# A mixture of experts with PE's order written out: two blocks interleaved by chunks, and the first layer's chunks in alternating PSUM banks

## The chip, the cores and the metric

One core of a Trainium2 chip runs the whole program in one launch. The metric is the time of one execution on the device in microseconds, as the median of several runs.

## The reference

The program is a network of four layers, each with a cross attention, a sequence block and a feed-forward block, on 16 x 64 = 1024 rows of 256 numbers, all in float32. The change touches only the feed-forward block of the second layer, a mixture of eight experts in which each row goes to its best two:

```
probs = softmax(xt @ gate_w.T)
top_w, top_i = top_k(probs, 2)
top_w = top_w / (top_w.sum(-1) + 1e-9)
h = gelu(einsum('td,ndh->tnh', xt, w1) + b1)       # 256 -> 1024
out_all = einsum('tnh,nhd->tnd', h, w2) + b2       # 1024 -> 256
out = (out_all at the chosen two, times top_w).sum(1)
```

The reference computes all experts for all rows; the kernel computes only the chosen ones.

## The kernel before, in words

The kernel is written on a layer that builds instructions for every engine, orders them by a scheduler, and sets the semaphores between engines from what each instruction reads and writes. `set_order(True)` and `in_order` add a chain between the instructions of one engine that are recorded through `mm`, `tr` or a `queue`, so that they stand in the order in which the program names them; without it the scheduler chooses the order.

`ffn1` (the method that the change edits) works so:

- The gate's logits, the two best experts of each row and the places of the rows are worked out by `choose` and by the lines after it. The 2048 choices (1024 rows times 2) are packed by expert into blocks of 128 places, with each expert's part rounded up to a whole block. NG = 23 blocks always suffice, and all 23 are computed. `whose` holds, for each block, which expert's weights it uses.
- `slots` turns places into lists: `src` (the row that stands at each place), `to` (where its result goes) and `weight`. Its matrix products are named `pi`, `pb`, `pw` and `pf`, and two of its inputs, `at` and `val`, are made on POOL.
- For each block, POOL issues indirect DMAs that gather the weights of the block's expert, `up` (128 x 2056, of which 8 columns are the bias) and `down` (128 x 2048), about 1 MB each, into three buffers each, and the block's 128 rows `xg` (`take`), also three buffers.
- `expert` then computes the block. Two transposes on PE put the rows into `pxg`, and DVE copies them to `xT`. The first layer's 1024 outputs are made in eight chunks of 128. A chunk is two products on PE (k = 0, 1) into its eighth of the PSUM tile `pu`, and one GELU on ACT from there into `hT` (L2631). The tile `pu` is 128 x 1024 float32, which is two PSUM banks: chunks 0 to 3 lie in the first and chunks 4 to 7 in the second. The second layer is eight products into `pd`, one for each chunk of `hT`. DVE scales the result by `weight` into `y` (L2637), and POOL scatters it to the table `d_y` in memory by an indirect DMA (L2642).
- A float32 product is two records in the profile, so a block has 32 `pu`, 16 `pd` and 2 `pxg` records on PE.
- There are two `pu` tiles (`big`, two buffers), and four PSUM buffers of one bank for `pxg`, `pd` and others (`mid`).
- The last block is not scattered. `add_sent` waits until all scatters have landed, loads the table back in eight pieces (`yk`, on SP's queue), adds the two halves of each on POOL, adds them to the residual `X` on DVE, and adds the last block by a product with a 0/1 matrix (`py`). The next stage begins with the statistics of `X`, and then transposes it (`psT`).

In the block loop the order is left to the scheduler: `set_order(False)` has been called at the end of `slots`. The scheduler puts the `pd` products of a block between its own `pu` chunks, and moves the next block's transposes and first chunks up into the present block. On POOL it issues the requests for `up`, `down` and `xg` in an order of its own; before the first block it puts two slot operations (L72 `at` and `val`) after the first three weight requests.

Of the kernel before, what the change touches and what calls it, by code (L numbers as in the profile page):

```python
# [8 lines left out]
F32 = mybir.dt.float32  # L9
U8 = mybir.dt.uint8  # L10
AF = mybir.ActivationFunctionType
ALU = mybir.AluOpType
# [3 lines left out]
P = 128  # L16
B, TQ, D = 16, 64, 256
N = B * TQ
# [37 lines left out]
def bc(ap, axis, n):  # L56

    ap = ap.unsqueeze(axis)
    shape = list(ap.shape)
    shape[axis] = n  # L60
    return ap.to_broadcast(shape)
# [17 lines left out]
class Net:  # L79
# [2663 lines left out]
            )  # L2743

    def ffn1(self):
        nc, a = self.nc, self.a
        L = "L1_ffn"

        NG = 2 * N // P + 7
        I32 = mybir.dt.int32  # L2750
        wg = self.w(a[f"{L}_gate_wT"].rearrange("(k p) n -> p k n", p=P), [P, 2, 8], "wg")
        with ExitStack() as es:
            one, two, big, mid = self.moe_pools(es, L)
            d_x, d_y = self.rows_dram(es, L)
            self.no_rows(d_y, one)
            row = self.numbers(one)
            comb = self.empty_combine(one)
            val = self.empty_values(NG, one)
            self.norm_T(mid, "m")
            p, oh, pq, seen, prod, gate = self.choose(wg, d_x, one, mid)  # L2760
            dve, pool = self.queue("dve", nc.vector), self.queue("pool", nc.gpsimd)

            pn = mid.tile([P, 512], F32, tag="m", name="pn")
            self.mm(pn[:, :8], self.ones, seen[:, :, 2 * NT - 1])
            over = one.tile([P, 8, 2 * NT], F32, name="over")
            fill, base, end = (one.tile([P, 8], F32, name=n) for n in ("fill", "base", "end"))
            below = one.tile([P, 8, 8], F32, name="below")
            dve.tensor_tensor(over, bc(self.nth[:, : 2 * NT], 1, 8), bc(pn[:, :8], 2, 2 * NT), ALU.is_lt)
            dve.tensor_reduce(fill, over, AX.X, ALU.add)
            dve.tensor_scalar(fill, fill, float(P), None, ALU.mult)  # L2770
            dve.tensor_tensor(below, self.lt8, bc(fill, 1, 8), ALU.mult)
            dve.tensor_reduce(base, below, AX.X, ALU.add)

            done = one.tile([P, NG, 8], F32, name="done")
            of = one.tile([P, NG], F32, name="of")
            whose = one.tile([P, NG], I32, name="whose")
            dve.tensor_tensor(end, fill, base, ALU.add)
            dve.tensor_tensor(done, bc(end, 1, NG), bc(self.nth[:, :NG], 2, 8), ALU.is_le)
            dve.tensor_reduce(of, done, AX.X, ALU.add)
            dve.tensor_scalar(of, of, 7.0, float(P), ALU.min, ALU.mult)  # L2780
            dve.tensor_scalar(whose, of, self.token[:, 0:1], -1.0, ALU.add, ALU.add)
            place = one.tile([P, 8, 2 * NT], F32, name="place")
            dve.tensor_tensor(place, pq, bc(base, 2, 2 * NT), ALU.add)
            r = self.over_both(p, gate, 1e-9, one)
            pool.tensor_tensor(comb[:, :, :8], prod[:, 0], prod[:, 1], ALU.add)
            pool.tensor_tensor(comb[:, :, :8], comb[:, :, :8], bc(r, 2, 8), ALU.mult)

            def weights(g):
                up = two.tile([P, 2048 + 8], F32, tag="up", name="up", bufs=3)
                down = two.tile([P, 8, D], F32, tag="down", name="down", bufs=3)  # L2790
                for t, name in ((up, "up"), (down.rearrange("p c d -> p (c d)"), "down")):
                    pool.indirect_dma_start(
                        out=t,
                        out_offset=None,
                        in_=a[f"{L}_{name}"],
                        in_offset=bass.IndirectOffsetOnAxis(ap=whose[:, g : g + 1], axis=0),
                    )
                return up, down

            first = weights(0)  # L2800
            xg, src, to, weight = self.slots(
                place, oh, r, gate, comb, val, 1, NG, one, big, mid, lambda src: self.take(src, 0, 1, d_x, two)
            )
            sent = []
            for g in range(NG):
                up, down = weights(g) if g else first
                if g:
                    xg = self.take(src, g, 1, d_x, two)
                wu = up[:, :2048].rearrange("p (k n) -> p k n", k=2)
                args = xg, 1, wu, down, up[:, 2048:], AF.Gelu, weight, to, g, d_y  # L2810
                if g < NG - 1:
                    self.expert(*args, sent, big, mid, two)
            self.add_sent(
                d_y, sent, lambda: self.expert(*args, None, big, mid, two), src, NG - 1, row, one, two, mid
            )

    def gate_up(self, e):

# [255 lines left out]
```

## Time and profile before

| | |
|---|---|
| median of 3 runs | 3036.7 us (3031.17 to 3040.3) |
| the profiled execution | 3037.57 us |
| its span, first to last instruction | 3035.9 us |
| mean granted clock of PE | 0.965 |
| PE busy (matmul) | 2884.4 us, 95% |
| DVE busy | 1952.2 us, 64% |
| ACT busy | 1329.5 us, 44% |
| POOL busy | 738.7 us, 24% |
| block loop of this stage, first transpose to end of the last y | about 1390.5 to 1578.0 us |

The profile is one execution, taken by the hardware's profiler. Times are microseconds from the first instruction. PE is the matrix engine and PEld its weight loads, DVE the vector engine, ACT the scalar engine, POOL the general engine that also issues the indirect DMAs, and SP the engine that issues others. A row of the timeline has the start, the time, the engine, the source line, the operation with `output<-input`, shapes, a count of equal instructions that follow each other, and in brackets how long the engine had been idle before and what ended that. L208 is the one line through which all recorded matrix products go, so the tile's name says which product it is. A row of the waits has who waited for what: total us, times, longest. A row of a stretch has, for each engine, busy us and the number of instructions, then PE's granted clock (1.00 is full), the DMA engines' share and GB/s. The starts of matrix products are recorded; their ends are modelled, so that products which overlap in the pipeline show longer times than their distance.

### The profile page before, as it was taken

Reading aid. Unit: us, or ns where it says so; the run is one execution under the profiler, and the core shown is the slowest. Engines: PE = TensorE matmul, PEld = TensorE weight load, DVE = VectorE, ACT = ScalarE, POOL = GpSimd, SP = SyncE. Lnnn points to the kernel's source line nnn. Section 1 sums busy time; section 2 is a strip of 40 time slices with the busy share of each in tenths; the row PEclk is TensorE's granted clock in tenths of the full one; section 3 lists DMA queues with packets and bytes.
Section 4 is the critical chain, followed back from the end, with each engine's and each line's share of the span. In section 5 each row is a group of like instructions: output and inputs, shape, how many; then the busy total and the mean of one; then the engine's idle time right before and its main releaser. Section 6 shows DMA issues by size and latency. Waiting matters only on the chain.

```text
span 3035.9 us, 65790 instructions
## 1 busy us (share of the span) xinstructions
PE 2884.4 (95%) x27660; PEld 1827.9 (60%) x27660; DVE 1952.2 (64%) x4059; ACT 1329.5 (44%) x3055; POOL 738.7 (24%) x817
## 2 busy tenths in 40 slices
PE   8999999999999999987989999998999899998888
PEld 4666666666555554466875555545985454545677
DVE  6888886524776665952127777767985667775521
ACT  4555554412554441002335444438951355554222
POOL 1000002400210001014430100025971454542132
PEclk9999999999999999968999999997999999999889
DMA  2010000014233313026862222101111211110243
GB/s 75 23 44 33 23 30 13 18 35 113 64 83 94 102 47 85 21 67 242 296 233 71 74 74 76 61 22 32 57 61 37 71 59 63 66 45 15 72 141 125
DMA packets 75760, 225.00 MB, mean 74 GB/s; under 512 B 17416, under 2 KB 30587, under 8 KB 68553
## 3 DMA queue, kind: packets, MB, share of 16 engines
q1 hardware_dynamic: 47536, 115.57, 12.6%
q0 software_dynamic: 21680, 99.08, 9.6%
q10 hardware_dynamic: 6248, 6.14, 0.7%
q8 instruction: 219, 3.59, 0.5%
q14 instruction: 77, 0.62, 0.1%
HBM read 209.83 MB, written 14.49 MB: 74 GB/s over the span
## 4 chain that ended last, share of the span: by engine, by line
PE 86%; DVE 7%; ACT 3%; POOL 2%; issue 1%; DMA 1%; SPq 0%; DVEq 0%; POOLq 0%; ACTq 0%
PE pss L208 15%; PE o L208 13%; PE pu L208 8%; PE pd L208 7%; PE psp L208 6%; PE pkv L208 5%; PE pst L211 4%; PE psc L208 4%; PE po L208 3%; PE pb L208 2%; PE psq L208 2%; PE py L1633 2%; PE psi L208 2%; PE psy L208 1%; PE pg L208 1%
## 5 line engine op out<-in xcount | busy, mean ns | idle before, releaser
L208 PE MATMUL pss<-cT,qw 128*32 128x256 f32 x8192 | 360.9, 381 | 5.7 <-ACT pr L72 5.7
L72 DVE TENSOR_REDUCE nm<-pss 128x2 f32<-128x512 f32 (+1 forms) x384 | 314.6, 861 | 68.5 <-PE pss L208 68.3
L208 PE MATMUL o<-pT,cx 128*64 128x512 f32 (+3 forms) x1088 | 351.7, 576 | 0.0
L72 ACT ACTIVATE pr<-pss,nmm 128x256 f32<-128x256 f32 x512 | 234.8, 485 | 151.1 <-DVE nmm L72 145.7
L208 PEld LDWEIGHTS pss<-cT,qw 128*32 128x32 f32 x8192 | 201.0, 108 | 133.2 <-issue 18.4
L225 POOL TENSOR_SCALAR rs<-mv 128x8 f32<-128x8 f32 (+3 forms) x50 | 10.1, 201 | 1084.3 <-DVE mv L243 609.7
L208 PEld LDWEIGHTS o<-pT,cx 128*64 128x64 f32 (+1 forms) x1088 | 134.3, 163 | 188.4 <-issue 167.1
L72 ACT ACTIVATE pr<-pr,sm 128x256 f32<-128x256 f32 x256 | 109.1, 497 | 192.2 <-DVE sm L72 192.2
L208 PE MATMUL pkv<-wx,cT 128*128 128x512 f32 (+1 forms) x512 | 190.7, 625 | 0.6 <-issue 0.6
L72 DVE TENSOR_SCALAR pr<-pr,sm 128x256 f32<-128x256 f32 (+1 forms) x384 | 169.5, 484 | 6.3
L211 PEld LDWEIGHTS pst<-ident,pr 128*128 128x128 f32 x1024 | 114.4, 141 | 69.2 <-DVE pr L72 25.0
L208 PE MATMUL pd<-wd,hT 128*128 128x256 f32 x656 | 151.6, 382 | 2.6 <-DVE hT L2879 1.4
L72 DVE STREAM_TRANSPOSE pT<-pr 128x1024 f32<-128x1024 f32 x128 | 151.8, 1224 | 2.2
L2637 DVE TENSOR_SCALAR y<-pd,row 128x256 f32<-128x256 f32 x39 | 18.9, 483 | 205.8 <-PE pd L208 205.8
L1626 POOL TENSOR_TENSOR h<-h,cb 128x1024 f32<-128x1024 f32 x63 | 147.2, 2379 | 15.1 <-DVE h L72 15.0
L72 DVE TENSOR_TENSOR_SCAN h<-dA,pb 128x512 f32<-128x512 f32 x128 | 145.3, 1201 | 5.4 <-PE pb L211 2.5
L72 ACT ACTIVATE pr<-pss,nm 128x1024 f32<-128x1024 f32 x128 | 142.0, 1118 | 2.9 <-DVE nm L72 2.9
L208 PEld LDWEIGHTS pd<-wd,hT 128*128 128x128 f32 x656 | 122.0, 190 | 30.3 <-DVE hT L2879 5.7
L211 PE MATMUL pst<-ident,pr 128*128 128x128 f32 x1024 | 136.0, 276 | 2.0 <-DVE pr L72 1.3
L208 PEld LDWEIGHTS pkv<-wx,cT 128*128 128x128 f32 (+1 forms) x512 | 63.6, 187 | 116.8 <-issue 90.4
L1857 POOL TENSOR_TENSOR rnk<-rnk,mhalf 128x8 f32<-128x8 f32 (+1 forms) x84 | 130.2, 1550 | 7.0
L72 ACT COPY pT<-pst 128x512 f32<-128x512 f32 x128 | 75.1, 587 | 127.4 <-PE pst L211 127.4
(572 smaller groups left out, 5843.2 us busy)
## 6 DMA issues: line engine op xcount, KB each, us to landing
cT<-in_ctxT SPq DMA_DIRECT2D x32, 768.0 KB, 4.2
cx<-in_ctxP SPq DMA_DIRECT2D x32, 768.0 KB, 4.2
cT<-in_ctxT SPq DMA_DIRECT2D x32, 512.0 KB, 4.1
cT<-in_ctxT SPq DMA_DIRECT2D x64, 256.0 KB, 4.9
offb<-d_off SPq DMA_DIRECT2D x16, 576.0 KB, 3.7
cb<-d_C SPq DMA_DIRECT2D x16, 512.0 KB, 3.6
wu<-in_L_ffn_w POOLq DMA_DIRECT2D x8, 1024.0 KB, 5.6
wd<-in_L_ffn_w POOLq DMA_DIRECT2D x8, 1024.0 KB, 6.3
```

The lines of the kernel that those rows point to most:

```text
L72: ins = getattr(self.engine, op)(*args, **kwargs)
L208: self.in_order(self.nc.tensor.matmul(out, lhsT=lhsT, rhs=rhs, start=start, stop=stop))
L211: self.in_order(self.nc.tensor.transpose(out, in_, self.ident))
L225: nc.gpsimd.tensor_scalar(t[:p, :n], in_, scale, eps, ALU.mult, ALU.add)
L1626: nc.gpsimd.tensor_tensor(hs[i], hs[i], cbs[hf, g], ALU.mult)
L1633: nc.tensor.matmul(py[:, t, ch], lhsT=x, rhs=self.ident, start=start, stop=stop, is_transpose=True, skip_group_check=True,)
L1857: nc.gpsimd.tensor_tensor(r, r, self.mhalf[:, : n * H], ALU.pow)
L2637: nc.vector.tensor_scalar(y[:, i, :], po[:, i * D : (i + 1) * D], weight[:, g + i : g + i + 1], None, ALU.mult)
```

## The change

The loop over `expert` is replaced by a loop written out in `ffn1` with PE's and POOL's order fixed (`set_order(True)`):

- Block 0's eight first-layer chunks run first (`widen(0, c)`). Then each turn g of the loop runs, for c = 0 to 7, chunk c of block g+1's first layer and chunk c of block g's second layer (`narrow(g, c)`). After chunk 4 stand the transposes of block g+2. The last block's second layer is left for `add_sent`.
- Chunk c of the first layer goes to place `c % 2 * 4 + c // 2` of the tile `pu`: even chunks into the first bank and odd ones into the second.
- The requests for `xg` and the weights are issued at fixed points: two blocks' weights before `slots`, `xg` and `up` of block g+3 at the start of turn g, and `down` of block g+3 after the scatter of block g.

The order of instructions as built: on PE, four `pu` records, two `pd`, four `pu` and so on through all 22 turns. On POOL, before the first block, `up`, `down`, `up`, `down`, `at`, `val`, `xg`; then in each turn `xg`, `up`, scatter, `down`. ACT has the same list as before. On DVE the last three scalings `y` stand ahead of the first `yk` addition, and a part of the next stage's statistics stands between the additions.

```diff
-            def weights(g):
-                up = two.tile([P, 2048 + 8], F32, tag="up", name="up", bufs=3)
-                down = two.tile([P, 8, D], F32, tag="down", name="down", bufs=3)
...
-            first = weights(0)
+            rows, ups, downs, xTs, hTs, pus, pds, ys = ({} for _ in range(8))
+
+            def weights(g, name):
...
+            for g in range(2):
+                for name in ("up", "down"):
+                    weights(g, name)
             xg, src, to, weight = self.slots(
                 place, oh, r, gate, comb, val, 1, NG, one, big, mid, lambda src: self.take(src, 0, 1, d_x, two)
             )
             sent = []
-            for g in range(NG):
-                up, down = weights(g) if g else first
-                if g:
-                    xg = self.take(src, g, 1, d_x, two)
-                wu = up[:, :2048].rearrange("p (k n) -> p k n", k=2)
-                args = xg, 1, wu, down, up[:, 2048:], AF.Gelu, weight, to, g, d_y
-                if g < NG - 1:
-                    self.expert(*args, sent, big, mid, two)
-            self.add_sent(
-                d_y, sent, lambda: self.expert(*args, None, big, mid, two), src, NG - 1, row, one, two, mid
-            )
+            rows[0] = xg
+            self.set_order(True)
...
+            def turn(g):
+                pt = mid.tile([P, 2, P], F32, tag="m", name="pxg")
+                for k in range(2):
+                    self.tr(pt[:, k, :], rows[g][:, 0, k * P : (k + 1) * P])
+                xTs[g] = two.tile([P, 2, P], F32, tag="xT", name="xT")
+                nc.vector.tensor_copy(xTs[g], pt)
+
+            def widen(g, c):
+                if c == 0:
+                    pus[g] = big.tile([P, 8, P], F32, tag="b", name="pu")
+                    hTs[g] = two.tile([P, 8, P], F32, tag="hT", name="hT")
+                wu = ups[g][:, :2048].rearrange("p (k n) -> p k n", k=2)
+                for k in range(2):
+                    self.mm(pus[g][:, c % 2 * 4 + c // 2, :], wu[:, k, c * P : (c + 1) * P], xTs[g][:, k, :], k == 0, k == 1)
+                nc.scalar.activation(
+                    hTs[g][:, c, :], pus[g][:, c % 2 * 4 + c // 2, :], AF.Gelu, bias=ups[g][:, 2048 + c : 2049 + c]
+                )
+
+            def narrow(g, c):
+                if c == 0:
+                    pds[g] = mid.tile([P, 512], F32, tag="m", name="pd")
+                self.mm(pds[g][:, :D], hTs[g][:, c, :], downs[g][:, c, :], c == 0, c == 7)
+
+            def send(g):
...
+            fetch(1)
+            fetch(2)
+            weights(2, "up")
+            weights(2, "down")
+            turn(0)
+            for c in range(8):
+                widen(0, c)
+            turn(1)
+            for g in range(NG - 1):
+                fetch(g + 3)
+                weights(g + 3, "up")
+                for c in range(8):
+                    widen(g + 1, c)
+                    narrow(g, c)
+                    if c == 4 and g + 2 < NG:
+                        turn(g + 2)
+                send(g)
+                weights(g + 3, "down")
+            self.set_order(False)
+
+            def last():
+                for c in range(8):
+                    narrow(NG - 1, c)
+                send(NG - 1)
+                return ys[NG - 1]
+
+            self.add_sent(d_y, sent, last, src, NG - 1, row, one, two, mid)
```

`send` holds the scaling, the scatter and the bookkeeping of `expert`; `fetch` calls `take`.

More of the change, by code (lines that the diff above doesn't have):

```diff
@@ L2745, in ffn1 @@
     def ffn1(self):
-        nc, a = self.nc, self.a
+        nc, tc, a = self.nc, self.tc, self.a
         L = "L1_ffn"
@@ L2786, in ffn1 @@
             pool.tensor_tensor(comb[:, :, :8], comb[:, :, :8], bc(r, 2, 8), ALU.mult)
-            def weights(g):
-                up = two.tile([P, 2048 + 8], F32, tag="up", name="up", bufs=3)
-                down = two.tile([P, 8, D], F32, tag="down", name="down", bufs=3)
[L2791 to L2796, printed above, removed]
-                    )
-                return up, down
-            first = weights(0)
+            rows, ups, downs, xTs, hTs, pus, pds, ys = ({} for _ in range(8))
+            def weights(g, name):
+                if g >= NG:
+                    return
+                if name == "up":
+                    t = ups[g] = two.tile([P, 2048 + 8], F32, tag="up", name="up", bufs=3)
+                else:
+                    downs[g] = two.tile([P, 8, D], F32, tag="down", name="down", bufs=3)
+                    t = downs[g].rearrange("p c d -> p (c d)")
+                pool.indirect_dma_start(
+                    out=t,
+                    out_offset=None,
+                    in_=a[f"{L}_{name}"],
+                    in_offset=bass.IndirectOffsetOnAxis(ap=whose[:, g : g + 1], axis=0),
+                )
+            for g in range(2):
+                for name in ("up", "down"):
+                    weights(g, name)
             xg, src, to, weight = self.slots(
@@ L2804, in ffn1 @@
             sent = []
-            for g in range(NG):
-                up, down = weights(g) if g else first
-                if g:
-                    xg = self.take(src, g, 1, d_x, two)
-                wu = up[:, :2048].rearrange("p (k n) -> p k n", k=2)
-                args = xg, 1, wu, down, up[:, 2048:], AF.Gelu, weight, to, g, d_y
-                if g < NG - 1:
-                    self.expert(*args, sent, big, mid, two)
-            self.add_sent(
-                d_y, sent, lambda: self.expert(*args, None, big, mid, two), src, NG - 1, row, one, two, mid
-            )
+            rows[0] = xg
@@ new lines, in ffn1, with fetch @@
+            self.set_order(True)
+            def fetch(g):
+                if g < NG:
+                    rows[g] = self.take(src, g, 1, d_x, two)
+            def turn(g):
[13 more added lines that the diff above has]
+                    hTs[g][:, c, :], pus[g][:, c % 2 * 4 + c // 2, :], AF.Gelu, bias=ups[g][:, 2048 + c : 2049 + c]
+                )
@@ new lines, in narrow @@
+            def narrow(g, c):
[3 more added lines that the diff above has]
+            def send(g):
+                y = ys[g] = two.tile([P, 1, D], F32, tag="y", name="y")
+                nc.vector.tensor_scalar(y[:, 0, :], pds[g][:, :D], weight[:, g : g + 1], None, ALU.mult)
+                if g == NG - 1:
+                    return
+                ins = nc.gpsimd.indirect_dma_start(
+                    out=d_y,
+                    out_offset=bass.IndirectOffsetOnAxis(ap=to[:, g : g + 1], axis=0),
+                    in_=y[:, 0, :],
+                    in_offset=None,
+                    bounds_check=2 * N - 1,
+                    oob_is_err=False,
+                )
+                self.in_order(ins, "pool")
+                for other in sent:
+                    tc.declare_no_dep(ins.ins, other, reason="one choice to a place")
+                sent.append(ins.ins.name)
```

## Prediction

> **What bounds the kernel now.** I first read the table of stretches over the block loop of the second mixture of experts, then its waits, then the order of time inside one block and at the loop's end.
>
> ```profile
> core 0: us, PE busy (x) PEld busy (x) DVE busy (x) ACT busy (x) POOL busy (x), PEclk, DMA share, GB/s
> 1410.00:1430.00 20.00, 20.00 (x127) 17.54 (x126) 2.73 (x6) 7.41 (x21) 9.71 (x10) 1.00 0.80 291
> 1450.00:1470.00 20.00, 20.00 (x127) 17.73 (x127) 2.30 (x5) 7.22 (x21) 10.49 (x11) 1.00 0.75 269
> ```
>
> PE looks full at full clock, but ends of matmuls are modelled; starts tell more.
>
> ```profile
> 1457.40 0.60 PE L208 MATMUL pd<-down,hT 128*128 128x256 f32 x2
> 1457.84 0.38 PE L208 MATMUL pu<-xT,up 128*128 128x128 f32 x2
> 1458.06 0.67 PE L208 MATMUL pd<-down,hT 128*128 128x256 f32 x2
> ```
>
> Start to start, two pd take 0.44 us and two pu 0.22. A block has 32 pu, 16 pd and 2 transposes (each f32 product is two records), so its bare work is 16 x 0.22 + 8 x 0.435 + 0.22 = 7.23 us. What it takes is the distance of the y scalings of two blocks:
>
> ```profile
> 1451.40 0.48 DVE L2637 TENSOR_SCALAR y<-pd,row 128x256 f32<-128x256 f32 x1 [6.04 <-PE pd L208]
> 1467.16 0.48 DVE L2637 TENSOR_SCALAR y<-pd,row 128x256 f32<-128x256 f32 x1 [6.04 <-PE pd L208]
> ```
>
> 15.76 / 2 = 7.88 us. So 0.65 us a block is lost, in this wait of the weight load:
>
> ```profile
> PEld pu L208 <- ACT hT L2631: 10.4, 40, 0.3
> ```
>
> The first product of a chunk waits for the GELU of the chunk before. The scheduler covers most of it with two first-layer products or a transpose of the next block. The loop's end, where no next block is left, shows the wait bare:
>
> ```profile
> 1570.47 0.37 ACT L2631 ACTIVATE hT<-pu,up 128x128 f32<-128x128 f32 x1 [0.80 <-PE pu L208]
> 1570.89 0.52 PEld L208 LDWEIGHTS pu<-xT,up 128*128 128x128 f32 x4 [0.43 <-ACT hT L2631]
> 1570.89 0.71 PE L208 MATMUL pu<-xT,up 128*128 128x128 f32 x4
> 1571.44 0.60 PE L208 MATMUL pd<-down,hT 128*128 128x256 f32 x2
> 1571.64 0.37 ACT L2631 ACTIVATE hT<-pu,up 128x128 f32<-128x128 f32 x1 [0.80 <-PE pu L208]
> 1572.06 0.52 PEld L208 LDWEIGHTS pu<-xT,up 128*128 128x128 f32 x4 [0.42 <-ACT hT L2631]
> 1573.23 0.71 PE L208 MATMUL pu<-xT,up 128*128 128x128 f32 x4
> 1574.40 0.71 PE L208 MATMUL pu<-xT,up 128*128 128x128 f32 x4
> 1575.57 0.71 PE L208 MATMUL pu<-xT,up 128*128 128x128 f32 x4
> ```
>
> Four pu, two pd, then the wait: a ring of 1.17 us a chunk. Its parts: 0.44 from the first to the fourth pu start (0.21 of it the first, whose weight load had to wait), 0.31 to the GELU, 0.37 of GELU, 0.05 back to PE. The last row is chunk 7 (only pd follow it), so 1570.89 is chunk 3 and 1572.06 chunk 4. Chunks 0 to 3 lie in one PSUM bank and 4 to 7 in the other, and yet this step, too, is 1.17 with a wait of 0.42: the wait is not for the bank.
>
> **The banks.** The change puts even chunks into one bank and odd ones into the other. By the crossing 3 to 4 this lifts no wait. The changed kernel as built agrees: the first pu of chunk c waits for the ACT count of the GELU of chunk c-1, not c-2, for c from 1 to 7; only chunk 0, in a fresh tile, has no such wait. Value: 0. (The Trainium skill, PSUM — Partial Sum Buffer, its summary of rules, has one guard PSUM by bank and read another bank than the one PE writes; by that rule the ring would be gone and a block 7.23 us. The crossing speaks against it here.)
>
> **The pinned order.** It is now: four pu of chunk c, two pd of the block before, next chunk; the two transposes stand after chunk 4. That is the loop's end of above, for all 22 turns; the next block's first products, which filled the gap, can no longer move up. Per turn: chunk 0 comes without a wait, so its ring is 1.17 - 0.10 = 1.07 (first pu 0.11 instead of 0.21); chunks 1, 2, 3 and 6 take 1.17 each; chunk 4 has the transposes, PE sets it: 0.55 + 0.435 + 0.22 = 1.20; chunk 5 starts without a wait, 1.07; chunk 7 is followed by an unwaiting chunk 0, 0.55 + 0.435 = 0.98. Sum 4.68 + 1.07 + 1.20 + 1.07 + 0.98 = 9.00 us, against 7.88. 22 turns: 198.0 us. Bounds 8.9 (chunk 4 and 5 better hidden) and 9.2 (chunks 4 and 5 at 1.17 and transposes on top).
>
> **The start.** Before, the first transpose starts at 1390.53. The second `down` request now stands on POOL ahead of the two slot products (L72 at, val), so `pi` starts later by its issue, some 1.5 us (1377.49 to 1379.0); so do `xg` and the two val products after it, and `pw` (3.64 us) ends at 1389.4 instead of 1387.85. But `xg` now has 4 MB of weights ahead of it and not 5, so it no longer comes last (9.46 us of landing before); `pw` does. First transpose 1389.5: -1.0 us (bounds -3.5, if xg and pw both come early, and +1.5). Then block 0's eight chunks run with no pd between them, at the half clock of the rows there:
>
> ```profile
> 1391.49 1.22 PE L208 MATMUL pu<-xT,up 128*128 128x128 f32 x4
> 1393.17 1.22 PE L208 MATMUL pu<-xT,up 128*128 128x128 f32 x4 [0.46 <-ACT hT L2631]
> ```
>
> 1.68 a chunk. Transpose to pu(0) 0.96, seven rings 11.8, the last four pu 0.9, turn of block 1 0.95: the loop starts at 1389.5 + 14.6 = 1404.1. At full clock the rings are 1.17: 4.2 less. Half clock held from 1391.4 to 1398.3 before, where PE was busier than it will be, so I take it as lasting through this piece, and charge 1.9 us for the loop's first chunks (1.9 each at half clock, as 1393.17 to 1395.04 shows, for some 5 us). Inside the loop I take full clock: the loop's end, with 0.88 of work in 1.17, keeps it.
>
> **The end.** The last scatter (L2642) went out at 1569.85 and the next stage's first transpose (psT) at 1589.40, 19.55 later, through the chain scatter, `yk` loads on SP, POOL's adds, DVE. Block 22's remaining work lay under that. It still does: after the loop only 16 pd are left, 3.5 us, under the 6.2 us from scatter to the first `yk` add. DVE has the last y and some statistics done earlier than before: -1.0 us (0 to -1.5).
>
> **At nothing.** 184 GELUs, 23 y and xT, and all DMAs are the same in number. POOL per turn: xg, up, scatter, down, 4 x 1.0 plus gaps = 5 us, under 9. Scatter and `down` wait for the end of the turn's pd, and the next xg and up are queued behind them; each has over a turn until PE needs it, against landings of 4.7 (xg; 9.5 at most) and 5.8 to 7.0 (weights). If that cover were gone, PE, now in fixed order, would stop for each late row.
>
> **The sum.** Loop end 1404.1 + 1.9 + 198.0 = 1604.0; y and scatter 1.0 later, 1605.0 against 1569.85: +35.1. With the end, +34.1. Profiled execution 3037.57 (span 3035.9): 3071.7. The median of runs is 0.9 lower, so 3071 us. Its own range: turns -2 to +4, start -7 to +3, end +1: 3062 to 3080.
>
> **Rivals.** (1) Faster: the chunk waits only for its own bank's GELU, two chunks back. Then 0.88 x 2 of PE work covers the ring, a turn is 7.23 and block 0 costs 8 x 0.89: loop from 1398.5, end 1398.5 + 2 + 159.1 = 1559.6, scatter 1560.6, -9.3, with the end -10.3: 3026. It decides if the chunk's distance falls under 1.0 (7.88 / 8). For it: the change's layout. Against it: the crossing and the built waits. 0.05. (2) The clock falls in the loop, PE having 20% of gaps: 1.9 a chunk instead of 1.13, up to +130, 3200. Against it: the loop's end. 0.04. (3) No change: rings overlap better than I see, chunk distance near 1.0: 3037 ± 9. 0.02. The forecast: 0.89.
>
> **The numbers.** 0.3% is 9 us, about what this measurement can tell from no change. Faster: rival 1 less its edge, 0.04; same 0.04; slower 0.92. The range 3061 to 3081 is the forecast's, widened by a microsecond for the runs' spread; it leaves out the rivals.
>
> **What would show it.** Right: four pu every 1.17 us through the loop, y every 9.0 us, PEld pu waiting for ACT hT some 5 times a block with up to 0.4 us each (about 40 us in all), the scatter at 1605. Wrong: a chunk every 0.88 us and y every 7.23 (rival 1); PEclk under 1.00 in the loop (rival 2); PE waiting for xg or up.

## The result, and the profile after

| | before | after |
|---|---|---|
| median of the runs | 3037.7 us (3031.17 to 3040.3, 4 runs) | 3069.43 us (3065.69 to 3071.51, 4 runs) |
| ratio | | 1.0119, 95% interval 1.0104 to 1.0133 |
| profiled execution | 3037.57 us | 3071.31 us |
| its span, mean granted clock | 3035.9 us, 0.965 | 3069.6 us, 0.962 |
| one block of the loop | 7.88 us | 9.115 us |
| first `up` request to the last scatter | 198.3 us | 236.4 us |
| first `up` request to the next stage's `psT` | 217.9 us | 254.3 us |

The change costs 1.2%. The last two rows are distances inside the stage, measured from the first weight request; what happens in the stages around it, which the change doesn't touch, is left out of them. That stage distance is the one on which the experiments below are compared. The ratio of each experiment is to runs of the kernel before that were taken along with it.

One execution of experiment 3's kernel, of seven, took 7263.65 us at a granted clock of 1.00, for a reason that nothing on record shows; its ratio leaves that one out.

The table of stretches of the changed kernel, in the middle of its loop (columns as before: busy us and count of PE, PEld, DVE, ACT, POOL, then PE's clock, DMA share, GB/s):

```profile
core 0: us, PE busy (x) PEld busy (x) DVE busy (x) ACT busy (x) POOL busy (x), PEclk, DMA share, GB/s
1410.00:1430.00 20.00, 19.59 (x111) 13.68 (x109) 1.82 (x4) 6.55 (x18) 9.16 (x10) 1.00 0.63 240
1450.00:1470.00 20.00, 19.62 (x113) 13.94 (x111) 2.24 (x5) 6.58 (x18) 8.44 (x9) 1.00 0.72 268
```

PE still looks 98% busy, but it runs some 112 matmul records in 20 us instead of 127. The weight loads show the gap better: PEld is busy for 13.9 us of 20 instead of 17.7. (The Trainium skill, Perfetto Trace Analysis, Identifying the Most-Contended Engine, says that the matmul busy share is a poor measure and sends the reader to the weight loads' share; these rows agree. Its reason is that pipelined matmuls look smaller in a trace; here their modelled ends make them look larger.) The clock is full and the DMA engines do less than before, so neither is the bound.

The timeline of the changed kernel inside a turn (`...` stands for rows left out):

```profile
1451.87 0.52 PEld L208 LDWEIGHTS pu<-xT,up 128*128 128x128 f32 x4 [0.42 <-ACT hT L2833]
1451.87 0.71 PE L208 MATMUL pu<-xT,up 128*128 128x128 f32 x4
...
1452.42 0.60 PE L208 MATMUL pd<-down,hT 128*128 128x256 f32 x2
1452.62 0.37 ACT L2833 ACTIVATE hT<-pu,up 128x128 f32<-128x128 f32 x1 [0.80 <-PE pu L208]
1453.04 0.52 PEld L208 LDWEIGHTS pu<-xT,up 128*128 128x128 f32 x4 [0.43 <-ACT hT L2833]
1453.04 0.71 PE L208 MATMUL pu<-xT,up 128*128 128x128 f32 x4
...
1454.22 0.48 DVE L2844 TENSOR_SCALAR y<-pd,row 128x256 f32<-128x256 f32 x1 [2.87 <-PE pd L208]
...
1463.34 0.48 DVE L2844 TENSOR_SCALAR y<-pd,row 128x256 f32<-128x256 f32 x1 [2.87 <-PE pd L208]
```

Four `pu`, two `pd`, then the wait for the GELU of the chunk just made, and the next chunk 1.17 us after the last: what the loop's end showed in the kernel before now fills the whole loop. The two scalings `y` are 9.12 us apart. The waits of the changed kernel over the loop:

```profile
PEld pu L208 <- ACT hT L2833: 53.3, 123, 0.5
```

Before, the same wait was 10.4 us in 40 cases. The loop's end in the changed kernel:

```profile
1597.21 0.61 PE L208 MATMUL pu<-xT,up 128*128 128x128 f32 x4
...
1597.66 1.03 PE L208 MATMUL pd<-down,hT 128*128 128x256 f32 x4
...
1598.52 0.61 PE L208 MATMUL pu<-xT,up 128*128 128x128 f32 x4
...
1600.91 0.48 DVE L2844 TENSOR_SCALAR y<-pd,row 128x256 f32<-128x256 f32 x1 [9.47 <-PE pd L208]
...
1601.78 0.48 DVE L2844 TENSOR_SCALAR y<-pd,row 128x256 f32<-128x256 f32 x1 [0.38 <-PE pd L208]
```

In the last turn there are four `pd` records between chunks, not two: the last block's own second layer, which is outside the fixed order, was put there by the scheduler. So chunks are 1.31 us apart, the last turn takes 9.96 us, and the last `y` follows the one before it by 0.87 us.

### The profile page after: what moved, and what is told of

The parts are those of the page before. It is cut to its first block, busy times and chain, and to the rows that moved or that the text cites. A ratio compares the mean times of both kernels' runs of the same rounds, so it can differ in the third digit from the quotient of the medians.

```text
span 3069.6 us, 65773 instructions
## 1 busy us (share of the span) xinstructions
PE 2908.8 (95%) x27660; PEld 1818.4 (59%) x27660; DVE 1950.8 (64%) x4059; ACT 1329.5 (43%) x3055; POOL 738.8 (24%) x817
## 3 DMA queue, kind: packets, MB, share of 16 engines
q1 hardware_dynamic: 47536, 115.57, 12.5%
## 4 chain that ended last, share of the span: by engine, by line
PE 85%; DVE 7%; ACT 3%; POOL 2%; issue 2%; DMA 1%; SPq 0%; ACTq 0%; DVEq 0%; POOLq 0%
PE pss L208 14%; PE o L208 13%; PE pu L208 9%; PE pd L208 7%; PE psp L208 6%; PE pkv L208 5%; PE pst L211 4%; PE psc L208 4%; PE po L208 2%; PE psq L208 2%; PE pb L208 2%; PE psi L208 1%; DVE h L72 1%; PE py L1633 1%; PE psy L208 1%
## 5 line engine op out<-in xcount | busy, mean ns | idle before, releaser
L208 PEld LDWEIGHTS pu<-xT,up 128*128 128x128 f32 x736 | 102.4, 197 | 63.3 <-ACT hT L2833 60.1
L208 PE MATMUL pu<-xT,up 128*128 128x128 f32 x736 | 132.4, 304 | 7.7 <-ACT hT L2833 3.2
L2833 ACT ACTIVATE hT<-pu,up 128x128 f32<-128x128 f32 x184 | 67.7, 368 | 148.6 <-PE pu L208 148.6
```

The source lines that it names most:

```text
L208: self.in_order(self.nc.tensor.matmul(out, lhsT=lhsT, rhs=rhs, start=start, stop=stop))
L2833: nc.scalar.activation(hTs[g][:, c, :], pus[g][:, c % 2 * 4 + c // 2, :], AF.Gelu, bias=ups[g][:, 2048 + c : 2049 + c])
```

## The experiments

Theories: **(A)** the wait follows the PSUM tile. All eight chunks write one tile, so the next chunk waits for the last GELU on it, whichever bank that read; the fixed order keeps the scheduler from filling the wait. **(B)** The wait follows the bank, and the loss comes from elsewhere in the new code (POOL's order, the late first block, the clock). "Stage" below is the distance from the first `up` request to `psT`, "turn" the mean distance of the `y` scalings.

**1. The changed kernel with its chunks in plain order in the tile.**

```diff
-  self.mm(pus[g][:, c % 2 * 4 + c // 2, :], ...)
+  self.mm(pus[g][:, c, :], ...)
```

> The changed kernel with the chunks of the first layer in their old places of the tile (0 to 3 in one bank, 4 to 7 in the other). Theory (the first product of a chunk waits for the GELU of the chunk before in the same tile, whatever the bank; the layout is worth nothing): a turn of the loop stays at 9.1 us, 3069 us as the changed kernel, ratio to before 1.010 to 1.013. Rival (the layout lifts some waits, and the pinned order cost more than the net shows): turns longer than 9.1 us, slower than 3075.

Measured: 3064.47 us (3063.16 to 3070.53), ratio to before 1.0101 (1.007 to 1.0132); turn 9.116, stage 254.5 against 254.3; the wait of PEld for `hT` is the same, 53.3 us in 123 cases. The new bank layout is worth nothing in the fixed order.

**2. The kernel before with the new layout.** The reverse test, in the scheduler's order.

```diff
+  at = (lambda j: j % 2 * 4 + j // 2) if per == HC and full == 1 else (lambda j: j)
-  self.mm(ps[:, c - c0, :], ...)
+  self.mm(ps[:, at(c - c0), :], ...)
```

> The kernel before with the layout by banks alone. Theory (layout worth nothing): two blocks in 15.76 us as before, ratio to before 1.000 within 0.002. Rival (the layout lifts every chunk's wait but one's): towards 7.25 us a block, up to 12 us faster.

Measured: 3032.89 us (3029.34 to 3037.5), ratio 0.9992 (0.9973 to 1.0011); turn 7.88, stage 216.3 against 217.9; the wait of PEld for `hT` is 10.4 us in 40 cases, as before. Nothing there either.

**3. The changed kernel with each block's even chunks in one tile and its odd chunks in another.** The order is that of the change, and even and odd chunks still lie in different banks. The addresses are not quite those of the change: a block now takes the first half of both `big` buffers, so every block writes the same two banks, where in the change two neighbouring blocks had a buffer each.

```diff
+  if c < 2:
+      pus[g, c] = big.tile([P, 8, P], F32, tag="b", name="pu")
-  self.mm(pus[g][:, c % 2 * 4 + c // 2, :], ...)
+  self.mm(pus[g, c % 2][:, c // 2, :], ...)
```

> The changed kernel with the even and the odd chunks in two tiles instead of two banks of one tile; order as in the changed kernel. Theory (the wait follows the tile): a chunk now waits for the GELU two chunks back, the ring of 1.17 us lies under two chunks of PE work (1.76), a turn falls from 9.11 to 7.25 us, block 0's chunks from 1.68 to 0.9 us at half clock, the time to about 3030 (3024 to 3038), the last block's products, which the scheduler moves into the last turn, included. Rival (the wait has another cause, or PE's fixed order costs by itself): turns stay near 9.1 us, 3069. Second rival (DMA ends it): turns between 7.4 and 7.9, PE waiting for up or xg.

Measured: median 3019.19 us, ratio 0.996 (0.9929 to 0.9992); turn 7.247, stage 203.3. The turn is the expected one; the time lies 5 us below the expected range. The timeline of this version:

```profile
1450.38 0.61 PE L208 MATMUL pu<-xT,up 128*128 128x128 f32 x4
...
1450.83 0.60 PE L208 MATMUL pd<-down,hT 128*128 128x256 f32 x2
1451.03 0.37 ACT L2834 ACTIVATE hT<-pu,up 128x128 f32<-128x128 f32 x1 [0.51 <-PE pu L208]
...
1451.26 0.61 PE L208 MATMUL pu<-xT,up 128*128 128x128 f32 x4
...
1455.19 0.48 DVE L2845 TENSOR_SCALAR y<-pd,row 128x256 f32<-128x256 f32 x1 [2.21 <-PE pd L208]
...
1462.44 0.48 DVE L2845 TENSOR_SCALAR y<-pd,row 128x256 f32<-128x256 f32 x1 [2.21 <-PE pd L208]
```

A chunk every 0.88 us: PE starts the next one 0.14 us before the GELU of the last (1451.03 + 0.37) ends. No row of its waits has PEld waiting for `hT`. Theory A holds and B falls. (One guards PSUM by bank, says the Trainium skill, PSUM — Partial Sum Buffer, Summary: rules for kernel authors. The runs show that a layout by bank alone does nothing where the waits are set per tile: runs 1 and 2 lack or have it without effect, and the gain comes once each of the two banks has a tile of its own. No run here has two tiles in one bank, so whether the bank matters besides the tile isn't shown.)

**4. The changed kernel with PE's order in the loop left to the scheduler** (POOL's order and the early requests stay).

```diff
-  self.mm(pus[g][:, c % 2 * 4 + c // 2, :], wu[...], xTs[g][:, k, :], k == 0, k == 1)
+  nc.tensor.matmul(pus[g][:, c % 2 * 4 + c // 2, :], lhsT=wu[...], rhs=xTs[g][:, k, :], start=k == 0, stop=k == 1)
```

(The same for `pd` and the transposes: what is recorded past `mm` and `tr` is not chained.)

> The changed kernel with PE's order left to the scheduler (POOL's order still fixed, layout by banks kept). Theory (what costs is the fixed order, in which no products of another block fill the ring): the scheduler moves the next block's first chunk under the last ring, a turn of 8.5 to 8.7 us, about 3058 (3050 to 3064). Rival (the cost comes from POOL's new order or from block 0 run alone): turns stay at 9.1, 3069.

Measured: 3020.8 us (3011.71 to 3026.05), ratio 0.9964 (0.9947 to 0.9981); turns of 6.87 and 8.06 in alternation, mean 7.464, stage 204.4. This was a miss: I had expected the scheduler to hide part of the ring, and it hides nearly all of it. Its timeline shows how:

```profile
1454.37 1.05 PE L2832 MATMUL pu<-xT,up 128*128 128x128 f32 x8
...
1455.01 0.86 ACT L2833 ACTIVATE hT<-pu,up 128x128 f32<-128x128 f32 x2 [0.94 <-PE pu L2832]
...
1455.26 0.60 PE L2840 MATMUL pd<-down,hT 128*128 128x256 f32 x2
...
1455.69 1.05 PE L2832 MATMUL pu<-xT,up 128*128 128x128 f32 x8
```

Eight `pu` are two chunks in one go, and two GELUs follow back to back. By theory A a tile lets only one chunk of its block through at a time, so these must be chunks of two blocks, whose rings run beside each other; the rows themselves don't name the block. With one tile a block the fixed order costs 9.115 - 7.464 = 1.65 us a turn, all of the loss and more. POOL's new order and the early requests are still in this version, whose stage is 13.5 us shorter than that of the kernel before: they are not what made the change slower.

**5. The changed kernel, each GELU issued twice.**

```diff
   nc.scalar.activation(hTs[g][:, c, :], ..., AF.Gelu, ...)
+  nc.scalar.activation(hTs[g][:, c, :], ..., AF.Gelu, ...)
```

> The changed kernel with every GELU of the loop issued twice (the same result written twice). Theory (the loop runs at the ring of four first-layer products, GELU and the way back): each ring grows by the second GELU, some 0.45 us, seven rings a turn: a turn of 12.2 to 12.5 us instead of 9.11, block 0 some 3 us longer, about 3140 us (3125 to 3160). Rival (PE's own work or its fixed order sets the turn, the GELU lies beside it): the turn stays at 9.1, 3069.

Measured (one run): 3130.82 us, turn 11.867. The timeline:

```profile
1449.82 0.71 PE L208 MATMUL pu<-xT,up 128*128 128x128 f32 x4 [0.42 <-ACT hT L2836]
...
1450.97 0.37 ACT L2836 ACTIVATE hT<-pu,up 128x128 f32<-128x128 f32 x1
1451.39 0.52 PEld L208 LDWEIGHTS pu<-xT,up 128*128 128x128 f32 x4 [0.83 <-ACT hT L2836]
1451.39 0.71 PE L208 MATMUL pu<-xT,up 128*128 128x128 f32 x4 [0.43 <-ACT hT L2836]
```

The ring grows from 1.17 to 1.57, by the 0.40 us at which the two GELUs of a chunk follow each other; I had taken 0.45, so the turn came out below the expected 12.2 to 12.5. The loop runs at ACT's answer, though ACT was busy for only a third of the changed kernel's loop (6.6 us of 20).

**6. Two tiles, each GELU issued twice**: run 3 with the edit of run 5.

> The kernel with two tiles, with every GELU issued twice. Theory (the ring now spans two chunks, 1.76 us of PE work, and hides up to 0.7 us more): a turn of 7.25 to 7.4 us, within 6 us of the two-tile kernel, ACT busy some 7.0 of 7.25 us. Rival (the two tiles gain by something else and a chunk still waits for its neighbour's GELU): a turn over 9.

Measured (one run): 3027.28 us, turn 7.404 from the third one on (7.25 to 7.58). From the first `y` to the twenty-second the added GELUs cost 2.8 us, against 56.9 us in run 5. The ring is still there; two chunks of distance hide most of it. Two parts of the expectation missed: ACT was busy for 15.6 us of 20, not for 7.0 of 7.25, and the stage is 7.6 us longer than in run 3, not within 6. Most of that, 4.6 us, had passed by the first `y`.

**7. The kernel before with two tiles.** Is the split alone enough?

```diff
+  if full == 1:
+      pss = {}
+      for c in range(HC):
+          if c < 2:
+              pss[c] = big.tile([P, per, W], F32, tag="b", name="pu")
...
```

> The kernel before with one edit: the even chunks of a block in one PSUM tile and the odd chunks in another, the order left to the scheduler. As built the scheduler answers with another order: three chunks, one pd product, two more chunks and so on, five pd products at the block's end, and the two transposes of the next block directly ahead of its first pu product, where before they stood inside the block. Theory: the tile split alone is not enough, since the block's seam is now bare: transpose to first pu was 0.96 us at the first block of before, of which 0.22 is work, and chunk 2 waits some 0.2 to 0.3 us for the GELU of chunk 0; a block then takes 7.23 + 0.75 + 0.25 = 8.2 us against 7.88, and the time is 3045 us (3037 to 3055). Rival: the seam is hidden behind the five pd products of the block before, a block takes 7.25 to 7.5 us, and the time is about 3025 us, so that the tiles alone bring the gain and the written-out order nothing.

Measured: 3048.25 us (3034.26 to 3055.85), ratio 1.0055 (1.0033 to 1.0077); turn 8.527, stage 227.8. PE's rows of the timeline:

```profile
1451.63 0.38 PE L2621 MATMUL pxg<-ident,xg 128*128 128x128 f32 x2
1452.70 1.93 PE L208 MATMUL pu<-xT,up 128*128 128x128 f32 x12 [0.69 <-DVE xT L2623]
1454.46 0.60 PE L208 MATMUL pd<-down,hT 128*128 128x256 f32 x2
```

The wait has moved to the seam of two blocks. From the transposes to the first `pu` it is 1.07 us, of which 0.22 is work; the twelve `pu` take 1.76 us and not 1.32. The third chunk waits for the GELU of the first, which is this row over the loop:

```profile
PEld pu L208 <- ACT hT L2634: 4.5, 18, 0.3
```

That is 0.25 us a block, as I had expected. The other 0.2 of the 0.44 us is the first record after each of the two waits, 0.21 us to the next start instead of 0.11. 0.85 + 0.44 = 1.29 us over the bare 7.23 gives 8.52. Direction and mechanism are as expected; what I had left out is the slower first record.

**8. Two tiles, PE's order left to the scheduler**: run 3 with the edit of run 4.

> The version with two PSUM tiles a block, but PE's order in the loop left to the scheduler (POOL's order and the early requests stay as in the changed kernel). As built the order is again one chunk, one pd product of the block before, with the transposes ahead of chunk 0. Theory: the interleaving follows from the order in which the program names the work and from the tiles, so fixing it buys nothing: 7.25 us a turn and 3019 us (3010 to 3030), as with the fixed order. Rival: the fixed order is worth something by itself, and without it a turn is 7.4 us or more and the time 3024 us or more.

Measured: 3009.77 us (3009.03 to 3025.47), ratio 0.9934 (0.9913 to 0.9955); turn 7.247, stage 200.7. The same turn as with the fixed order, and the stage 2.6 us shorter, since block 0 is done sooner (first `y` 30.6 us after the first request, 33.3 in run 3). Part of that may be the clock: half clock ended 0.3 us after the first `pu` here, and 3.9 us after it in run 3. So in the loop the fixed order buys nothing: the interleaving comes from the order in which the program names chunks, and from tiles that allow it. This version has the shortest stage found and is faster than both kernels; against run 3 the intervals overlap.

**9. Two tiles, the second block's weights requested after the first rows** (the last block's products are fixed too, which leaves PE's order as in run 3).

```diff
-  for g in range(2):
-      for name in ("up", "down"):
-          weights(g, name)
+  for name in ("up", "down"):
+      weights(0, name)
...
   fetch(1)
+  weights(1, "up")
+  weights(1, "down")
```

> The two-tile kernel with block 1's weights requested after the slots instead of before them. Theory: the two slot operations on POOL come 2.4 us earlier, and with them pi, pw and the first transpose (first transpose 15.0 us after the first up request instead of 17.5); the loop stays at 7.25 a turn; 2.4 us less than the two-tile kernel in the stage. Rival (the weights of block 1 then come late and PE waits in turn 0): no gain or some us lost.

Measured: 3021.99 us (3016.02 to 3033.16), ratio 0.9951 (0.993 to 0.9972); turn 7.247, stage 206.0, which is 2.7 us longer than run 3. The first transpose does come earlier, 15.3 us after the first request and not 17.5, as expected. But the first `pu` comes at 21.0, later than run 3's 18.9:

```profile
1379.69 0.69 PE L211 MATMUL pxg<-ident,xg 128*128 128x128 f32 x2
...
1384.14 0.37 ACT L72 COPY rows<-pw 128x256 f32<-128x256 f32 x1 [18.80 <-remote]
1384.19 0.42 DVE L2823 COPY xT<-pxg 128x256 f32<-128x256 f32 x1 [7.43 <-remote]
```

By the modelled ends of PE's products, ACT's and DVE's copies have their inputs by 1380.5; they start at 1384.1, on a releaser that the view calls remote. Both wait for PE's semaphore, and by the trace's record of its updates PE's signals for `pw` and `pxg` came at 1384.12 and 1384.16, 4.4 and 3.8 us after those ends; in run 3 they came within 0.05 us of them. So the pause lies between PE's products and their signals. It takes back the gain. What causes it wasn't settled; the rival's cause doesn't show, since no row of the waits in the first turns has PE waiting for `up` or `down`.

## Why the prediction was right, point by point

The forecast was 3071 us and the median 3069.4. The steps on the profiled executions:

- **The banks, value 0: right, and shown.** Run 1 has the fixed order without the layout and run 2 the layout without the fixed order, and each equals its partner within the intervals. The rule of the page, taken as it stands, would have given 7.23 us. Only the versions with two tiles and interleaved chunks (runs 3, 8 and 9) came to that, by an edit that the change lacks. Rival 1 had the right sum for them: its turn of 7.23 came out as 7.25 once a chunk no longer waited for the GELU of the chunk before.
- **The pinned order, 9.00 us a turn: measured 9.115.** The mechanism is shown by runs 3, 4 and 5. The term was 2.5 us too small over 22 turns: a chunk that begins without a wait saves 0.03 to 0.06 us and not 0.10, so that chunk 0 takes 1.11 and chunk 5 takes 1.14 where the sum had 1.07 for both. The others are as summed (1.17 four times, 1.20, 0.98).
- **The count of waits: a slip.** "Some 5 times a block", about 40 us, came out as 53.3 us. Chunks 1, 2, 3, 4, 6 and 7 wait, six a turn; the price of the rings had them all, so the time was not touched. Before, the same row has 10.4 us over some 20 blocks, 0.5 us a block; so it doesn't hold all of the 0.65 us that the prediction puts down to it.
- **The end: one sentence wrong.** "After the loop only 16 pd are left, 3.5 us": the scheduler moved them into the last turn. That lengthened it by 0.84 us, ahead of the last scatter, and spared nothing, since the 3.5 us had cover. The distance from scatter to `psT` fell by 1.7 us where 1.0 was put.
- **The start.** The first transpose came 1.6 us earlier after the first request (1.0 predicted). From there to the loop it took 15.3 us, not 14.6. Most of that is the first `pu`, which came 1.43 us after the transpose and not 0.96. Two `pf` products stand ahead of it in both kernels; but this stretch had full clock before (1388.0 to 1391.4) and half clock here, and `pf` first waited for ACT's copy of `pw`, which before was done over 2 us earlier. Block 0's rings are 1.68 us at half clock, as charged:

```profile
1385.85 1.22 PE L208 MATMUL pu<-xT,up 128*128 128x128 f32 x4 [0.46 <-ACT hT L2833]
...
1387.53 1.22 PE L208 MATMUL pu<-xT,up 128*128 128x128 f32 x4 [0.46 <-ACT hT L2833]
```

  Half clock ended at 1401.7, and cost the loop's first chunks 1.2 us where 1.9 was put. (The prediction's "4.2 less" at full clock is too much for its seven rings: 7 x 0.51 = 3.6. It bore only on the lower end of the range.)
- **At nothing: right.** No wait for `xg`, `up` or a free buffer shows on PE in the loop.

The stage grew by 254.3 - 217.9 = 36.4 us, against 34.1 predicted; the terms above differ by -0.6, +0.7, -0.7, +2.5, +0.8 and -0.7, which is +2.0 of these 2.3. The profiled executions differ by 33.7. The rest lies outside the stage. The first `up` request comes 6.2 us earlier: from 1290 us up to it, the kernel before ran 62.0 us at half clock and the one after 48.9. What follows the stage is 3.6 us longer. So the total's difference came out 1.9 us closer to the forecast than the stage's. That is luck, and no merit of the sum.

## What to carry to other kernels

Look up what a wait is set on before moving data about: here it was the tile, so a layout over two banks did nothing until each bank had a tile of its own, and then the same order took 1.87 us a block less. Do not fix an order ahead of the waits: here the fixed order paid a round trip between engines at nearly every chunk, where the scheduler filled most of it from another block; and once the waits were right, fixing bought nothing. One split without the other edit can lose as well (run 7), so test the pair, and compare the distance from start to start, since PE looked 98 to 100% busy at 7.25, 7.88 and 9.12 us a block alike.

## What the runs showed of the hardware beyond what was expected

- The runs' spread goes with the granted clock. The eight runs of experiment 7 go from 3034.26 us at a mean clock of 0.971 to 3055.85 at 0.963, those of experiment 8 from 3009.03 at 0.968 to 3025.47 at 0.963. The stretches at half clock lie in other places in each profile, also in stages that no edit touches (27.3 us from 1306.2 after, 47.8 us from 1295.9 before). A difference of under 10 us between single profiles is not readable from the total. The stage's distance is the better measure, though half clock falls in different places there too (experiment 8).
- A PE that waits for a fifth of its time in gaps of 0.4 us kept full clock through the whole loop of the changed kernel; the half-clock charge fell only on its start.
- The pause of some 4 us in experiment 9, between two of PE's products and their signals, is open. A shorter one shows in experiments 5 and 6: the same signals come 1.6 us after the modelled ends, and the first `pu` 20.4 us after the first request instead of 18.9.
